# Work on the first and last item of a batched attention and graph-convolution kernel, moved between engines and queue positions

## The chip, the cores and the metric

The kernel runs on one core of a Trainium2 chip. A core has five engines, each with its own instruction queue, which it works through in order: TensorE (PE, matrix products, with PEld for its weight loads), VectorE (DVE), ScalarE (ACT), GpSimd (POOL) and SyncE (SP), which here only starts transfers. They meet through semaphores. The metric is the device time of one execution in microseconds (us); lower is better.

## The reference

There are 32 items of 512 rows and 512 columns, one adjacency matrix of 512 x 512 shared by all, three projections, a weight and biases. Each item goes through masked attention with 8 heads of 64 columns, a residual addition and a layer norm without gain, then through a graph convolution, another residual addition and another layer norm:

```python
q = (x @ Wq + bq).reshape(b, n, H, HD)          # the same for k and v
scores = jnp.einsum('bihd,bjhd->bhij', q, k) / jnp.sqrt(HD)
scores = scores + jnp.where(adj == 0, -1e9, 0.0)
out = jnp.einsum('bhij,bjhd->bihd', softmax(scores), v)
x = layernorm(x + out)
norm_adj = adj * deg_inv_sqrt[:, None] * deg_inv_sqrt[None, :]
x = layernorm(x + einsum('nm,bmo->bno', norm_adj, x @ W1) + b1)
```

## The kernel before

Everything is in the function `unshifted`; the function `general` behind it runs only if a flag, counted at the end, says that the softmax without a running maximum lost accuracy. All engines are wrapped so that their instructions stay in the order in which the program issues them. The profile gives the wrapper's line, L40, for all of these, so the operations are told apart by the names of their tiles.

*Products.* Each of the three projections is done as seven block products instead of eight (`seven`): the weight and the transposed item are kept as four 256-row or 256-column parts and three further sums and differences. `weigh` makes those of a weight (four operations on 128x512 elements), `turns` transposes an item in two halves on VectorE (`turn`, tile xT from x) and then makes the item's combinations (`combine`, four operations; on VectorE for the first item, on GpSimd for all later ones). The products go in the order (0,0), (1,1), (5,5), (6,6), (4,4), (3,2), (2,3), part of the weight first, part of the item second. So the first two need no combination, and the third needs the second result of `weigh` and of `combine`. Each piece is eight TensorE instructions of 256 columns into one of three PSUM buffers (mm), which VectorE or ScalarE must empty. `values_of(b)` gives the values of an item, `keys_and_queries(b, r)` for r = 0, 1 its keys and queries, in which each piece holds four instructions for wk and four for wq.

*Attention.* An item has eight steps: four pairs of heads, two halves of keys. A step k issues `scores` of step k (eight TensorE instructions into two PSUM buffers sc, then on VectorE a minimum and the mask, on ScalarE the exponent, on GpSimd the sum over keys in acc) and `values` of step k-1 (eight instructions into av; VectorE transposes every second one into yb, and small transfers bring it into yT). The exponents lie in four buffers named e. One holds until its value product and its GpSimd sum are done. `sums` turns acc into column sums (sT) with small matmuls after half of the heads and after all of them.

*After the attention.* `finish(b)` is a list of 19 pieces: the reciprocals of the sums, four scalings of yT on VectorE with residual additions on GpSimd (yT from xr), four statistics, the root on GpSimd, and then for each of four row blocks the norm, a high part hi on ScalarE, a low part lo on VectorE and the addition of the bias on GpSimd. `convolve(b)` is a list whose first four pieces (the first factor, 8 instructions each, with hi and lo against adjT) give zT, and whose other eight are the four second factors (8 instructions against w) with their norm and their stores.

*Order.* The main loop runs over all 256 steps and two more. From the third step of each item on, a list `side` of pieces is spread over eight steps: the projections of the next item, `finish` and `convolve` of the one before, and the transposes of the one after next. A piece carries a cost, and `run(side, share)` issues pieces until their costs reach the share that is due. `weave(side, main)` spreads one list between the pieces of another. Pieces of `finish` have the cost 0, except the first with 0.6, so a list of nothing else is not spread: all but its first piece waits for the last step, where the share is 1. That is what happens in the last item:

```python
            else:
                side, late = finish(b - 1), convolve(b - 1)
...
    run(weave(finish(B - 1), late))
    run(convolve(B - 1))
```

So in the last item's attention TensorE has scores and values alone; then come the rest of item 30's `finish`, then item 31's `finish` woven into item 30's `convolve`, and last item 31's `convolve`. The flag is counted behind all that.

At the start the program issues, in this order: the transposes and combinations of item 0; the additional parts of Wv on VectorE; the value and key biases; the parts of Wk on GpSimd; item 0's values; the scale of 1/8 on Wq and its parts on VectorE; item 0's keys and queries; the transposes of item 1; then `adjacency`, which in four rounds transposes the adjacency matrix on TensorE and makes from it on VectorE the mask (maskT), a rounded copy (adjT), and a check (off, lost), and last the degrees (deg, root, dis). Then the steps begin. A buffer holds one half of an item before its transposition (x), so the load of the second half of item 1 can begin only when the first is transposed. The adjacency matrix lies in one of two yT buffers until the degrees are read from it.

Of the kernel before, what the change touches and what calls it, by code (L numbers as in the profile page):

```python
# [9 lines left out]
F32 = mybir.dt.float32  # L10
# [3 lines left out]
AF = mybir.ActivationFunctionType  # L14
ALU = mybir.AluOpType
AX = mybir.AxisListType

P = 128
# [3 lines left out]
MASKED = -1e9  # L22
# [23 lines left out]
def unshifted(  # L46
# [25 lines left out]
    nc = tc.nc  # L72
    B, N, D = x.shape
    NT = N // P
    DT = D // P
    G = H // 2
    SCALE = 1.0 / HD**0.5
    tensor, vector, scalar, gpsimd = (InOrder(tc, e) for e in (nc.tensor, nc.vector, nc.scalar, nc.gpsimd))
# [53 lines left out]
    def load_parts(w, name, engine):  # L132
        t = consts.tile([P, 7, 2, HALF], F32, name=name)
        for i in range(2):
            for q in range(4):
                engine.dma_start(
                    t[32 * q : 32 * (q + 1), 2 * i : 2 * i + 2].rearrange("r j u o -> r (j u) o"),
                    w[ts(q, P), ts(i, HALF)].rearrange("(t r) o -> r t o", r=32),
                )
        return t  # L140

    def weigh(t, engine):
        engine.tensor_tensor(t[:, 4], t[:, 2], t[:, 3], ALU.add)
        engine.tensor_tensor(t[:, 5], t[:, 4], t[:, 0], ALU.subtract)
        engine.tensor_tensor(t[:, 6], t[:, 0], t[:, 2], ALU.subtract)
        engine.tensor_tensor(t[:, 2], t[:, 1], t[:, 5], ALU.subtract)
# [3 lines left out]
        nc.sync.dma_start(t, w.rearrange("(t p) o -> p t o", p=P))  # L150
        return t

    def load_row(v, name):
        t = consts.tile([P, v.shape[0]], F32, name=name)
        nc.sync.dma_start(t, bass.AP(tensor=v.tensor, offset=v.offset, ap=[[0, P], [1, v.shape[0]]]))
        return t

    def load_column(v, name):
        t = consts.tile([P, DT], F32, name=name)
        nc.sync.dma_start(t, v.rearrange("(t p) -> p t", p=P))  # L160
        return t

    load_x(0, 0)
    load_x(0, 1)
    wv = load_parts(Wv, "wv", nc.scalar)
    bk_c = load_column(bk, "bk_c")
    bq_c = load_column(bq, "bq_c")
    wk = load_parts(Wk, "wk", nc.sync)
    wq = load_parts(Wq, "wq", nc.sync)
    bv_r = load_row(bv, "bv_r")  # L170
    adj_sb = acts.tile([P, NT, N], F32, name="yT")
    nc.sync.dma_start(adj_sb, adj.rearrange("(t p) o -> p t o", p=P))
    w1 = load_weight(W1, "w1")
    b1_r = load_row(b1, "b1_r")

    ident = consts.tile([P, P], F32, name="ident")
    make_identity(nc, ident)
# [9 lines left out]
    dis = consts.tile([P, NT], F32, name="dis")  # L187
    lost = consts.tile([P, NT], F32, name="lost")

    def adjacency():  # L190

        for m in range(NT):
            p = ps_mm.tile([P, N], F32, name="mm")
            for n in range(NT):
                tensor.transpose(p[:, ts(n, P)], adj_sb[:, n, ts(m, P)], ident)
            vector.tensor_scalar(maskT[:, m, :], p, 0.0, MASKED, op0=ALU.is_equal, op1=ALU.mult)
            vector.tensor_copy(adjT[:, m, :], p)
            off = work.tile([P, N], F32, name="off", tag="e", bufs=4)  # L200
            vector.tensor_tensor(off, p, adjT[:, m, :], ALU.not_equal)
            vector.tensor_reduce(lost[:, m : m + 1], off, AX.X, ALU.add)
        deg = consts.tile([P, NT], F32, name="deg")
        vector.tensor_reduce(deg, adj_sb, AX.X, ALU.add)
        pos = consts.tile([P, NT], F32, name="pos")
        vector.tensor_scalar(pos, deg, 0.0, None, op0=ALU.is_gt)
        safe = consts.tile([P, NT], F32, name="safe")
        vector.tensor_scalar(safe, deg, TINY, None, op0=ALU.max)
        root = consts.tile([P, NT], F32, name="root")
        gpsimd.tensor_tensor(root, safe, minus_half, ALU.pow)  # L210
        vector.tensor_mul(dis, root, pos)
# [44 lines left out]
    def values_of(b):  # L256


        def multiply(p, i, j):
            for r in range(2):  # L260
                for u in range(2):
                    tensor.matmul(
                        p[:, r, :], XT[b][:, j, u, ts(r, P)], wv[:, i, u, :],
                        start=u == 0, stop=u == 1,
                    )

        def first(e1, p):
            V[b] = acts.tile([P, NT, D], F32, name="v")
            vector.tensor_add(e1, p, bv_r[:, None, :HALF].to_broadcast([P, 2, HALF]))

        def middle(u2, u1, p):
            vector.tensor_add(u2, u1, p)
            vector.tensor_add(u2, u2, bv_r[:, None, HALF:].to_broadcast([P, 2, HALF]))

        def out(i, j):
            return V[b][:, 2 * j : 2 * j + 2, ts(i, HALF)]

        return seven(multiply, first, middle, out)

    def keys_and_queries(b, r):  # L280


        def multiply(p, i, j):
            for c, w in enumerate((wk, wq)):
                for u in range(2):
                    tensor.matmul(
                        p[:, c, :], w[:, i, u, ts(r, P)], XT[b][:, j, u, :],
                        start=u == 0, stop=u == 1,
                    )

        def first(e1, p):
            for g in (r, r + 2):
                KQ[b, g] = acts.tile([P, 2, N], F32, name="kq", bufs=5)
            for c in range(2):
                scalar.activation(e1[:, c], p[:, c], AF.Identity, bias=bias[:, c, r : r + 1], scale=1.0)

        def middle(u2, u1, p):
            for c in range(2):
                vector.scalar_tensor_tensor(
                    u2[:, c], u1[:, c], step[:, c, r : r + 1], p[:, c], op0=ALU.add, op1=ALU.add  # L300
                )

        def out(i, j):
            return KQ[b, r + 2 * i][:, :, ts(j, HALF)]

        return seven(multiply, first, middle, out)

    def turns(b):

        return [(0, turn, (b, 0))], [(0, turn, (b, 1))] + [(0, combine, (b, k)) for k in range(4)]  # L310
# [145 lines left out]
    def weave(side, main):  # L456

        out, done = [], 0
        for k, piece in enumerate(main):
            due = len(side) * (k + 1) // len(main)  # L460
            out += side[done:due] + [piece]
            done = due
        return out + side[done:]
# [39 lines left out]
    def run(pieces, share=1.0):  # L503

        due = share * sum(c for c, _, _ in pieces)
        done = 0
        while pieces and (done < due or share == 1.0):
            c, f, args = pieces.pop(0)
            f(*args)
            done += c  # L510
# [2 lines left out]
    steps = [(b, g, jj) for b in range(B) for g in ORDER for jj in range(2)]  # L513
    S = len(steps)
    PER = 2 * G
    for piece in sum(turns(0), []):
        piece[1](*piece[2])
    weigh(wv, vector)
    value_biases()
    biases()  # L520
    if B > 1:
        load_x(1, 0)
    weigh(wk, gpsimd)
    run(values_of(0))
    vector.tensor_scalar(wq[:, :4], wq[:, :4], SCALE, None, op0=ALU.mult)
    weigh(wq, vector)
    run(keys_and_queries(0, 0))
    run(keys_and_queries(0, 1))
    run(sum(turns(1), []) if B > 1 else [])
    adjacency()  # L530
    side, late = [], []
    for k in range(S + 2):
        b, at = divmod(k, PER)
        if at == 2:
            run(side)
            if b:
                for i in range(NT):
                    load_residual(b - 1, i)
            if b + 2 < B:
                load_x(b + 2, 0)  # L540
            side = []
            if b + 1 < B:
                side = values_of(b + 1) + keys_and_queries(b + 1, 0) + keys_and_queries(b + 1, 1)
            if b == 0:
                side = side + (sum(turns(2), []) if B > 2 else [])
            elif b < B - 1:
                chain = finish(b - 1)
                side = chain[:1] + side[:1] + weave(chain[1:], side[1:])
                one, two = turns(b + 2) if b + 2 < B else ([], [])
                conv = convolve(b - 1)  # L550
                side = side + one + conv[:4] + weave(two, conv[4:])
            else:
                side, late = finish(b - 1), convolve(b - 1)
        if k >= 2:
            pb, pg, pj = steps[k - 2]
            if pj == 1 and pg in ORDER[1::2]:
                sums(pb, ORDER.index(pg) // 2)
        if k < S:
            scores(steps[k])
        if 1 <= k <= S:  # L560
            values(steps[k - 1])
        run(side, 1.0 / (PER - (at - 2) % PER))
# [1 line left out]
    for i in range(NT):  # L564
        load_residual(B - 1, i)
    run(weave(finish(B - 1), late))
    run(convolve(B - 1))

# [8 lines left out]
    tensor.matmul(p, count, ones, start=True, stop=True)  # L579
    bad = small.tile([1, 1], I32, name="bad")  # L580
    vector.tensor_scalar(bad, p, -1.0, float(P * B * NT * H), op0=ALU.mult, op1=ALU.add)
    return nc.values_load(bad, min_val=0, max_val=P * B * NT * H + N * N)


# [280 lines left out]
```

## Time and profile before

| quantity | value |
|---|---|
| median of three runs | 3025.76 us (3025.0 to 3026.0) |
| span of the profiled execution | 3025.3 us |
| TensorE busy | 2957.3 us, 98% |
| VectorE busy | 2188.4 us, 72% |
| GpSimd busy | 1557.6 us, 51% |
| ScalarE busy | 775.9 us, 26% |
| mean granted TensorE clock | 0.988 |
| mean HBM traffic | 35 GB/s |

Busy time is the time in which an engine has an instruction in work. A share of the span is a mean over stages of different kinds, and the first and the last item differ from the 30 between. The page also gives the span in 40 equal slices of 75.6 us, with one digit for each (tenths, 9 for 90% or more), and the clock that TensorE was granted. Timeline rows give the start, the duration (for merged rows that from the first to the last instruction), the engine, the operation, its tiles, the count, and in brackets the idle time ahead with what ended it.

### The profile page before, as it was taken

The page shows a single profiled execution, that of the slowest core. Times are in us where ns is not written, and L with a number is a line of the kernel's source. Part 1 is how long each engine was busy: PE and PEld are TensorE (multiplying, and loading weights), DVE is VectorE, ACT ScalarE, POOL GpSimd, SP SyncE. Part 2 cuts the span into 40 slices and gives each one's busy share as a digit, 9 for nine tenths or more (in the row PEclk, how much of TensorE's full clock was granted, in tenths as well). Part 3 has the DMA queues.
Part 4 walks back from the last instruction along what each step waited for, and adds up shares of the span by engine and source line. Part 5 has one row for each costly group of instructions (what it writes and reads, how often), then busy time and mean ns, then how long its engine had stood idle before and what let it go on. Part 6 is the DMA issues. An engine that isn't in the chain of part 4 may idle for free.

```text
span 3025.3 us, 33347 instructions
## 1 busy us (share of the span) xinstructions
PE 2957.3 (98%) x12178; PEld 1721.9 (57%) x12178; DVE 2188.4 (72%) x3146; ACT 775.9 (26%) x929; POOL 1557.6 (51%) x939
## 2 busy tenths in 40 slices
PE   6899999999999999999999999999999999999996
PEld 5465555655555655556655556555556555556533
DVE  5577767777767777767877767877677777677756
ACT  0222222222222222222222222222222222222231
POOL 1355554555544555554555455555545555445553
PEclk8999999999999999999999999999999999999997
DMA  5012221122221112211222211122211222211121
GB/s 125 11 29 53 53 56 28 42 49 53 53 53 28 46 46 56 53 42 32 50 48 56 53 32 41 46 53 53 56 28 42 49 53 53 54 28 46 40 51 40
DMA packets 382861, 142.28 MB, mean 47 GB/s; under 512 B 280032, under 2 KB 348640, under 8 KB 382688
## 3 DMA queue, kind: packets, MB, share of 16 engines
q1 hardware_dynamic: 381536, 139.01, 19.8%
q8 instruction: 98, 1.61, 0.2%
q10 hardware_dynamic: 1152, 1.05, 0.2%
q14 instruction: 75, 0.61, 0.1%
HBM read 72.88 MB, written 33.55 MB: 35 GB/s over the span
## 4 chain that ended last, share of the span: by engine, by line
PE 96%; DVE 2%; DMA 1%; POOL 1%; issue 0%; SPq 0%; ACT 0%; DVEq 0%; POOLq 0%; ACTq 0%
PE mm L40 64%; PE sc L40 16%; PE av L40 15%; DMA x<-in_x_dram 1%; POOL acc L40 0%; DVE yT L40 0%; DVE st L40 0%; DVE e L40 0%; DVE ob L40 0%; DVE lo L40 0%; DMA bv_r<-in_L_gnn_bv_dram 0%; POOL rstd L40 0%; DMA wq<-in_L_gnn_Wq_dram 0%; SPq L105 0%; DVE xT L40 0%
## 5 line engine op out<-in xcount | busy, mean ns | idle before, releaser
L40 ACT ACTIVATE e<-e 128x1024 f32<-128x1024 f32 x512 | 541.2, 1057 | 1375.8 <-DVE e L40 1357.1
L40 POOL TENSOR_TENSOR acc<-acc,e 128x1024 f32<-128x1024 f32 x256 | 635.1, 2481 | 465.6 <-ACT e L40 455.4
L40 DVE SCALAR_TENSOR_TENSOR e<-sc,maskT 128x1024 f32<-128x1024 f32 x512 | 601.6, 1216 | 291.4 <-PE sc L40 290.2
L40 POOL TENSOR_TENSOR acc<-e 128x1024 f32<-128x1024 f32 x128 | 311.3, 2432 | 580.7 <-ACT e L40 529.9
L40 PE MATMUL sc<-kq 64*128 64x512 f32 x2048 | 512.6, 619 | 8.8 <-DVE e L40 8.8
L40 PE MATMUL av<-e,v 128*64 128x512 f32 x2048 | 496.6, 606 | 0.0
L40 PE MATMUL mm<-xT,wk 128*128 128x256 f32 x1792 | 469.8, 385 | 0.0
L40 PE MATMUL mm<-xT,wq 128*128 128x256 f32 x1792 | 460.0, 379 | 1.1 <-DVE wq L40 1.1
L40 PE MATMUL mm<-w,zT 128*128 128x512 f32 x1024 | 455.8, 598 | 0.0
L40 PE MATMUL mm<-wv,xT 128*128 128x256 f32 x1792 | 410.8, 387 | 19.2 <-DVE xT L40 9.5
L40 PEld LDWEIGHTS mm<-xT,wk 128*128 128x128 f32 x1792 | 332.6, 190 | 118.5 <-DVE e L40 26.8
L40 PEld LDWEIGHTS mm<-wv,xT 128*128 128x128 f32 x1792 | 338.8, 193 | 95.4 <-DVE u L40 23.5
L40 PEld LDWEIGHTS mm<-xT,wq 128*128 128x128 f32 x1792 | 340.4, 190 | 47.7 <-DVE wq L40 1.5
L40 PEld LDWEIGHTS mm<-w,zT 128*128 128x128 f32 x1024 | 189.6, 190 | 264.1 <-issue 237.5
L40 PEld LDWEIGHTS sc<-kq 64*128 64x128 f32 x2048 | 177.1, 187 | 264.3 <-issue 204.8
L40 PEld LDWEIGHTS av<-e,v 128*64 128x64 f32 x2048 | 124.2, 136 | 341.9 <-issue 315.4
L40 DVE SCALAR_TENSOR_TENSOR ob<-mm,dis,yT 128x512 f32<-128x512 f32 x128 | 96.1, 751 | 223.4 <-PE mm L40 223.3
L40 POOL TENSOR_TENSOR rstd<-ve,minus_half 128x1 f32<-128x1 f32 (+1 forms) x160 | 116.8, 730 | 217.7 <-DVE ve L40 214.3
L40 PE MATMUL mm<-adjT,hi 128*128 128x512 f32 x512 | 207.6, 406 | 10.3 <-ACT hi L40 10.3
L40 PE MATMUL mm<-adjT,lo 128*128 128x512 f32 x512 | 204.8, 400 | 7.4 <-DVE lo L40 7.4
L40 POOL TENSOR_TENSOR yT<-yT,b_r 128x512 f32<-128x512 f32 x128 | 170.5, 1332 | 78.3 <-DVE lo L40 78.3
L40 POOL TENSOR_TENSOR xT<-xT 128x512 f32<-128x512 f32 x124 | 158.7, 1280 | 53.5 <-DVE xT L40 51.0
(71 smaller groups left out, 2329.6 us busy)
## 6 DMA issues: line engine op xcount, KB each, us to landing
x<-in_x_dram SPq DMA_DIRECT2D x256, 128.0 KB, 2.9
xr<-in_x_dram SPq DMA_DIRECT2D x128, 256.0 KB, 2.7
yT<-yb SPq DMA_DIRECT2D x512, 64.0 KB, 2.4
out_dram<-ob SPq DMA_DIRECT2D x128, 256.0 KB, 2.0
wv<-in_L_gnn_Wv_dram ACTq DMA_DIRECT2D x8, 128.0 KB, 4.8
wk<-in_L_gnn_Wk_dram SPq DMA_DIRECT2D x8, 128.0 KB, 4.1
wq<-in_L_gnn_Wq_dram SPq DMA_DIRECT2D x8, 128.0 KB, 4.4
yT<-in_adj_dram SPq DMA_DIRECT2D x1, 1024.0 KB, 7.4
```

The lines of the kernel that those rows point to most:

```text
L40: return self.tc.keep_in_program_order(op(*args, **kwargs))
```

## The change

At the start, the additional parts of Wv are made on GpSimd, ahead of those of Wk; the scaling of Wq is done on ScalarE; the value bias is loaded through ScalarE's queue behind Wv, instead of SyncE's queue behind Wq, and its difference and the other biases are made after the first two value pieces; the parts of Wq are made behind the first key piece. The four rounds of `adjacency` are woven between the pieces of the second half of keys and queries, and the degrees become a piece of their own in the first item's side list. The second half of item 1's transposes and its combinations are issued behind the first scores.

At the end, the pieces of item 30's `finish` get a cost of 0.5 each, so that they spread over the attention of item 31, followed by the four first-factor pieces of its `convolve`. The second-factor pieces are held back until after the attention, with item 31's `finish` woven between them. The flag's count is placed ahead of item 31's `convolve`. The aim is to give TensorE work where it waits.

```diff
     load_x(0, 1)
     wv = load_parts(Wv, "wv", nc.scalar)
+    bv_r = load_row(bv, "bv_r", nc.scalar)
...
-    bv_r = load_row(bv, "bv_r")
...
-    def adjacency():
-        for m in range(NT):
-            p = ps_mm.tile([P, N], F32, name="mm")
...
+    def adjacency(m):
+        p = ps_mm.tile([P, N], F32, name="mm")
...
+    def degrees():
         deg = consts.tile([P, NT], F32, name="deg")
...
-    for piece in sum(turns(0), []):
-        piece[1](*piece[2])
-    weigh(wv, vector)
+    weigh(wv, gpsimd)
+    run(sum(turns(0), []))
+    weigh(wk, gpsimd)
+    scalar.activation(wq[:, :4], wq[:, :4], AF.Copy, scale=SCALE)
+    first = values_of(0)
+    run(first[:2])
     value_biases()
     biases()
     if B > 1:
         load_x(1, 0)
-    weigh(wk, gpsimd)
-    run(values_of(0))
-    vector.tensor_scalar(wq[:, :4], wq[:, :4], SCALE, None, op0=ALU.mult)
+    run(first[2:])
+    masks = [(0, adjacency, (m,)) for m in range(NT)]
+    first = keys_and_queries(0, 0)
+    run(first[:1])
     weigh(wq, vector)
-    run(keys_and_queries(0, 0))
-    run(keys_and_queries(0, 1))
-    run(sum(turns(1), []) if B > 1 else [])
-    adjacency()
+    run(first[1:])
+    run(weave(masks, keys_and_queries(0, 1)))
+    one, two = turns(1) if B > 1 else ([], [])
+    run(one)
...
             if b == 0:
-                side = side + (sum(turns(2), []) if B > 2 else [])
+                side = side[:7] + [(0, degrees, ())] + side[7:] + (sum(turns(2), []) if B > 2 else [])
...
             else:
-                side, late = finish(b - 1), convolve(b - 1)
+                conv = convolve(b - 1)
+                side = [(0.5, *piece[1:]) for piece in finish(b - 1)] + conv[:4]
+                late = conv[4:]
...
             scores(steps[k])
+        if k == 0:
+            run(two)
...
     run(weave(finish(B - 1), late))
-    run(convolve(B - 1))
...
     vector.tensor_scalar(bad, p, -1.0, float(P * B * NT * H), op0=ALU.mult, op1=ALU.add)
+    run(convolve(B - 1))
     return nc.values_load(bad, min_val=0, max_val=P * B * NT * H + N * N)
```

More of the change, by code (lines that the diff above doesn't have):

```diff
@@ L151, in load_weight, with load_row @@
         return t
-    def load_row(v, name):
+    def load_row(v, name, engine):
         t = consts.tile([P, v.shape[0]], F32, name=name)
-        nc.sync.dma_start(t, bass.AP(tensor=v.tensor, offset=v.offset, ap=[[0, P], [1, v.shape[0]]]))
+        engine.dma_start(t, bass.AP(tensor=v.tensor, offset=v.offset, ap=[[0, P], [1, v.shape[0]]]))
         return t
@@ L173, in unshifted @@
     w1 = load_weight(W1, "w1")
-    b1_r = load_row(b1, "b1_r")
+    b1_r = load_row(b1, "b1_r", nc.sync)
     ident = consts.tile([P, P], F32, name="ident")
@@ L188, in unshifted @@
     lost = consts.tile([P, NT], F32, name="lost")
-    def adjacency():
-        for m in range(NT):
-            p = ps_mm.tile([P, N], F32, name="mm")
[L196 to L202, printed above, removed]
+    def adjacency(m):
+        p = ps_mm.tile([P, N], F32, name="mm")
+        for n in range(NT):
+            tensor.transpose(p[:, ts(n, P)], adj_sb[:, n, ts(m, P)], ident)
+        vector.tensor_scalar(maskT[:, m, :], p, 0.0, MASKED, op0=ALU.is_equal, op1=ALU.mult)
+        vector.tensor_copy(adjT[:, m, :], p)
+        off = work.tile([P, N], F32, name="off", tag="e", bufs=4)
+        vector.tensor_tensor(off, p, adjT[:, m, :], ALU.not_equal)
+        vector.tensor_reduce(lost[:, m : m + 1], off, AX.X, ALU.add)
+    def degrees():
         deg = consts.tile([P, NT], F32, name="deg")
```

## The prediction

> **What bounds the kernel now.** I read the page's busy times first, then the slices, then the busy times of stretches that I cut at the places where the slices fall, and last the timeline of those stretches. The page:
>
> ```profile
> PE 2957.3 (98%) x12178; PEld 1721.9 (57%) x12178; DVE 2188.4 (72%) x3146; ACT 775.9 (26%) x929; POOL 1557.6 (51%) x939
> ...
> PE   6899999999999999999999999999999999999996
> ...
> PEclk8999999999999999999999999999999999999997
> ```
>
> TensorE is busy for 98% of the span and sits idle for 3025.3 - 2957.3 = 68 us in all. From the third slice to the last but one it never drops below 9. So whatever is changed in the 30 middle items is worth nothing unless it slows TensorE; the change can only earn in the first 95 us and the last 110 us. The stretches (columns: stretch, its length, busy us of PE, PEld, DVE, ACT, POOL with the number of instructions, granted clock, DMA share, GB/s):
>
> ```profile
> 0.00:9.00 9.00, 0.00 (x0) 0.00 (x0) 0.85 (x1) 0.00 (x0) 0.97 (x10) 1.00 0.89 168
> 9.00:38.30 29.30, 21.18 (x60) 16.21 (x60) 17.90 (x25) 1.10 (x1) 6.49 (x4) 0.77 0.99 235
> 38.30:61.70 23.40, 23.39 (x108) 20.58 (x109) 11.80 (x19) 1.86 (x5) 0.00 (x0) 1.00 0.00 1
> 61.70:95.00 33.30, 16.49 (x57) 6.10 (x55) 23.03 (x29) 5.38 (x6) 13.12 (x8) 0.69 0.13 32
> 2915.60:2943.50 27.90, 25.33 (x108) 7.05 (x104) 17.03 (x19) 13.27 (x13) 21.20 (x9) 1.00 0.34 69
> 2943.50:2962.00 18.50, 5.49 (x14) 2.36 (x15) 16.09 (x29) 2.78 (x4) 10.77 (x8) 0.60 0.24 68
> 2962.00:2992.30 30.30, 24.71 (x65) 13.62 (x63) 25.17 (x49) 5.24 (x8) 15.91 (x13) 0.84 0.05 18
> 2992.30:3015.40 23.10, 22.99 (x59) 13.07 (x59) 8.35 (x17) 2.35 (x4) 5.12 (x5) 0.87 0.10 39
> ```
>
> At the head TensorE loses 9 us to the first loads, 8 us in the value products (9 to 38), and 17 us between 61.7 and 95, where VectorE makes the masks. The clock column says that the work beside those gaps also runs slowly. At the tail 13 us are lost where the norm of item 30 runs alone (2943.5 to 2962), 6 us beside the norm of item 31, and 10 us behind the last product. The timeline shows what each head gap waits for:
>
> ```profile
> 26.36 10.03 PE L40 MATMUL mm<-wv,xT 128*128 128x256 f32 x32 [3.16 <-DVE e L40]
> ...
> 68.18 1.25 DVE L40 STREAM_TRANSPOSE xT<-x 128x1024 f32<-128x1024 f32 x1 [4.42 <-DMA x<-in_x_dram]
> 69.35 0.65 DVE L40 TENSOR_SCALAR maskT<-mm 128x512 bf16<-128x512 f32 x1
> ...
> 71.47 1.09 PE L40 MATMUL mm<-ident,yT 128*128 128x128 f32 x4 [8.15 <-DVE off L40]
> ...
> 72.49 3.79 PE L40 MATMUL sc<-kq 64*128 64x512 f32 x8
> ...
> 83.66 2.35 DVE L40 SCALAR_TENSOR_TENSOR e<-sc,maskT 128x1024 f32<-128x1024 f32 x2
> ...
> 84.93 3.79 PE L40 MATMUL sc<-kq 64*128 64x512 f32 x8 [8.66 <-DVE e L40]
> ...
> 91.27 1.99 PE L40 MATMUL sc<-kq 64*128 64x512 f32 x8
> ```
>
> The reader is to see VectorE as one queue in which everything stands in line: the second turn of item 1 waits 4.42 us for its load, the four masks behind it wait too, and the first softmax step (83.66) behind those. The eight score matmuls take 3.79 us after each gap and 1.99 us later.
>
> **What the Trainium skill says.** "TensorE: Matmul & The Clock Gate", Part 1: about 3.4 us without work drop the array's clock to half, and about as much work restores it. The trace agrees: 3.79 against 1.99 us for one and the same group after gaps of 8.15 and 8.66 us. "SBUF — State Buffer", Who interferes with whom: a VectorE operation with two SBUF inputs and a GpSimd operation that reads SBUF exclude each other. The trace agrees in part: the four differences of Wv on VectorE took 0.69 to 1.76 us while GpSimd worked on Wk, the same operation on Wq with GpSimd idle 0.69 us. "TensorE: Matmul & The Clock Gate", Part 1, also has VectorE and ScalarE as strict first-in-first-out; the chain above behaves so.
>
> **The head, part by part.** (1) Wv to GpSimd, bv on the other DMA queue. VectorE loses 4.76 us of Wv work. The last Wv load is issued at 7.8 us and lands within 3.2 to 5.6 us, so GpSimd starts near 13; at the 1.65 us of the Wk rows it is done near 19.6, and its second result, which the third value piece needs, near 16.3. VectorE's four x combinations (2.75 us alone, from 15.3) now run beside that; with exclusion they end at 19 to 21 instead of 18.0. The third piece starts near 17.5 (was 19.4); bv no longer arrives at 23.8, so the first eviction comes at about 20 to 21 (was 25.6) and the fourth piece at about 21 (was 26.4). The rest took 9.7 us, from 26.36 to 36.0, partly at half clock; with a shorter gap ahead I take 8.5 us: the keys start at 29.5 instead of 36.0.
> (2) Scaling Wq on ScalarE. The row for 128x2048 is 1.22 us on VectorE; for ScalarE no row exists: 1.06 us for 1024 columns and 0.42 for 256 give about 2 us. ScalarE is idle to 37 us, so this costs nothing, and the stall of 1.05 us before the queries goes. The Wq differences (2.75 us) follow the first key product, hidden by two pieces of 1.72 us. Wk on GpSimd ends near 26.5, before its first use near 33.
> (3) First half of keys and queries: 7 pieces of 1.72 us, 29.5 to 41.5.
> (4) Second half with the masks between. TensorE has 12.0 us plus 16 transposes, about 2 us. VectorE has four masks of 2.75 us (11.0) and seven evictions of about 0.7 (5.0): 16.0 us from about 43.9, so VectorE sets the end, at 59.9. The second half took 11.6 us before, so weaving costs 4 to 5 us here, and removes 21 us later.
> (5) First turn of item 1 (1.25): softmax from 61.2, against 83.66. The second turn now stands behind the first scores. Its load begins only after the first turn and needs 4.4 us and an issue, so VectorE waits until about 65.8, then turns, and the second scores are masked from 67.1 (was 87.06). GpSimd's four combinations (5.2 us) stand behind the first sum; they are wanted near 75 and done near 72. The exponents of the second step end at 70.6 and its value products at 72.5, which ended at 95.05: 22.5 us earlier. TensorE idles some 3 to 4 us at 58 to 62 and may cool: I take off 1 us. Head: 21.5 us.
> (6) Degrees, 2.3 us and five small operations, go into item 0's steady part, where VectorE has a quarter of its time free and their result is first used an item later: nothing.
>
> **The tail.** (7) The norm of item 30 (19 pieces) now runs beside the attention of item 31, and its four first factors follow in the last four steps. GpSimd decides this: from 2919.1 to 2943.5 it does nine sums of 2.36 us, 21.2 us with only 3.2 us of gaps. Four residual additions of 1.30, one root of 1.02 and four bias additions of 1.33 add 11.5 us. Queued behind them are the sums of exponents, and behind those the four score buffers (VectorE) and the column sums (TensorE). So the last column sums go from 2943.5 to at least 2955.0; I take 2956.5. Then 1.05 + 1.8 (the last first factor, 8 x 0.228) + 0.66 + 0.34 us bring the reciprocals of item 31 to 2960.4, where they were at 2961.98. All the 18.5 us of lonely norm are thus mostly repaid in a longer attention: 1.6 us earned.
> (8) The norm of item 31 beside the second factors. VectorE: four scalings of 1.40, four statistics of 1.01, four evictions with statistics of 1.77, three stores of 0.54, 0.56 of judging, four norms of 0.54 to 1.15, four splits of 0.74 to 0.90: 24 to 27 us, plus about 1.6 us for the first second factor and 1 us for the root. I take 28, where it took 30.3: 2.3 us earned.
> (9) The flag's count goes ahead of the last convolution. Its matmul waits for VectorE (a store and three small operations, 1.2 us) and all 32 matmuls of the first factors stand behind it; before, 7 of them had run by the last split. 1.2 + 7 x 0.228 = 2.8 us lost. Behind the last store the 0.6 us from count to flag are saved. Tail: 1.6 + 2.3 - 2.8 + 0.6 = 1.7 us.
>
> **Sum:** 3025.8 - 21.5 - 1.7 = 3002.6, say 3002.5.
>
> **Rivals.** A, the above. B: the tail pays as it was meant to. If GpSimd's additions fall into its gaps and behind waits, and the last norm needs VectorE's 24 us alone, the tail earns 10 to 12 us: about 2992. For it: TensorE idles 13 us there; against: 21.2 of 24.4 us of GpSimd are taken. C: the tail costs. Two-input scalings on VectorE shut out the sums (means of 1.40 instead of 0.69 show it), the attention of item 31 ends at 2960 or later and TensorE goes cold before the last convolution: 5 to 7 us lost, about 3010. D: the head is bound by its loads. The DMA share is 0.99 to 38 us; if Wv or bv lands as late as before and the masks wait for the adjacency, only the 8 to 10 us at 62 to 84 remain: 3015 to 3020, no change to speak of. E, slower: the head earns nothing, because the second turn's wait moves onto the first softmax steps and all their products run at half clock, and the tail loses the 11.5 us in full: about 3035. Against it: the masks' 11 us are then still done beside products.
>
> **How the numbers follow.** A 0.60, B 0.20, C 0.13, D 0.04, E 0.03. The range takes A with its unknowns (keys start 28 to 31, attention end 2955 to 2959) and reaches to B and C: 2991 to 3012. Faster by more than 0.2% means under 3019.7: A, B, C and part of D, 0.95; within 0.02; slower 0.03.
>
> **What would show it.** Head right: keys start near 29.5 us, VectorE without gaps from 44 to 60, the first softmax step near 61, the second turn waiting some 4 us for its load, and value products of the second step ending near 72.5. Tail right: GpSimd busy without gaps in the last attention, the last column sums some 13 us later in that stage, and the norm of item 31 beginning about 1.6 us earlier relative to the stage's start. A long TensorE gap before the last convolution shows step 9. If TensorE in the middle items shows gaps that are not there now, all of this is wrong.

## The result and the profile after

| kernel | median | runs | ratio to before, 95% interval |
|---|---|---|---|
| before | 3025.92 us | 6 (3025.0 to 3027.36) | |
| changed | 3005.45 us | 6 (3002.76 to 3006.53) | 0.9931 (0.9918 to 0.9944) |

The change saves about 20.5 us, 0.7%. The profiled executions differ by 21.3 us (spans of 3025.3 and 3004.0). The page after, busy times and slices:

```profile
PE 2949.8 (98%) x12178; PEld 1720.2 (57%) x12178; DVE 2190.6 (73%) x3141; ACT 777.2 (26%) x930; POOL 1561.5 (52%) x943
...
PE   7999999999999999999999999999999999999986
...
PEclk9999999999999999999999999999999999999998
```

The first slice went from 6 to 7 and the second from 8 to 9, and the first one's clock from 8 to 9; at the end the last slice but one fell from 9 to 8, while the last one's clock rose from 7 to 8. TensorE now idles 3004.0 - 2949.8 = 54.2 us instead of 68. The saving is larger than that difference of 14 us, since the work beside the closed gaps also runs faster (TensorE is busy 7.5 us less with the same 12178 instructions). The busy times of stretches of the changed kernel, cut at its own stages (columns as in the prediction):

```profile
9.00:29.90 20.90, 17.10 (x57) 13.60 (x58) 16.91 (x18) 3.20 (x2) 11.60 (x8) 0.92 1.12 259
29.90:43.70 13.80, 13.80 (x65) 12.13 (x64) 8.19 (x13) 0.84 (x2) 0.00 (x0) 1.00 0.44 109
43.70:57.30 13.60, 12.62 (x67) 10.64 (x65) 12.52 (x21) 0.84 (x2) 0.00 (x0) 1.00 0.00 1
57.30:72.00 14.70, 11.63 (x42) 3.23 (x41) 11.65 (x12) 5.72 (x6) 7.28 (x5) 0.88 0.29 72
2893.70:2938.60 44.90, 34.43 (x128) 11.85 (x124) 39.17 (x46) 17.11 (x19) 35.59 (x18) 0.89 0.29 65
2938.60:2942.20 3.60, 3.60 (x22) 2.35 (x22) 0.69 (x2) 1.02 (x2) 0.00 (x0) 1.00 0.53 73
2942.20:2971.70 29.50, 13.70 (x32) 5.71 (x30) 23.64 (x53) 2.92 (x5) 14.92 (x13) 0.82 0.08 32
```

**Head.** From 29.9 to 57.3 us TensorE works almost without a gap, from 44 us on beside VectorE making the masks; the value products of item 0's second step end, and item 1's products begin, at 71.99 instead of 95.06: 23.1 us earlier. The timeline of the changed kernel at that place:

```profile
21.20 8.86 PE L40 MATMUL mm<-wv,xT 128*128 128x256 f32 x32 [1.99 <-DVE e L40]
...
59.70 1.24 DVE L40 STREAM_TRANSPOSE xT<-x 128x1024 f32<-128x1024 f32 x1
60.86 2.31 DVE L40 SCALAR_TENSOR_TENSOR e<-sc,maskT 128x1024 f32<-128x1024 f32 x2
...
62.10 3.21 PE L40 MATMUL sc<-kq 64*128 64x512 f32 x8 [2.84 <-DVE e L40]
...
65.52 1.25 DVE L40 STREAM_TRANSPOSE xT<-x 128x1024 f32<-128x1024 f32 x1 [2.35 <-DMA x<-in_x_dram]
66.69 2.32 DVE L40 SCALAR_TENSOR_TENSOR e<-sc,maskT 128x1024 f32<-128x1024 f32 x2
```

The reader is to see the two waits that stood here, 8.15 us for the check of the adjacency and 8.66 us for the softmax, gone or cut to 2.84 us, and the wait of the second turn (2.35 us) now behind the first softmax step.

**Middle.** The lead of 23.1 us has become 21.8 by 200 us and is 21.9 at the last item. Both kernels have one wait of TensorE there, about 3 us, before a group of 16 products; the group took 5.26 us before and 6.59 after, so 1.3 us were lost. The experiments show below that this length varies with no change in the code.

**Tail.** The softmax of the last item's third step begins 21.9 us earlier (2915.62 and 2893.71), and the end comes 21.3 us earlier. So the tail costs 0.6 us. Cut at the starts of the named operations, for the last split at its end:

| from, to | before | changed | earned |
|---|---|---|---|
| third step's softmax, reciprocals of item 31 | 46.4 us | 48.5 | -2.1 |
| reciprocals, last split of item 31 | 30.9 | 27.9 | 3.1 |
| last split, last eviction | 22.4 | 26.0 | -3.5 |
| last eviction, end | 10.0 | 8.0 | 2.0 |

The waits of TensorE in the changed kernel, by what ended them (us in total, times, longest), and three rows of the tail's timeline:

```profile
PE mm L40 <- DVE ones L40: 15.8, 1, 15.8
PE sc L40 <- DVE e L40: 12.6, 6, 5.8
PE mm L40 <- DVE xT L40: 10.8, 2, 9.6
PE mm L40 <- DVE inv L40: 3.0, 1, 3.0
```

```profile
2896.98 6.79 DVE L40 TENSOR_TENSOR yT<-yT,inv 128x512 f32<-128x512 f32 x4
...
2904.95 3.78 PE L40 MATMUL sc<-kq 64*128 64x512 f32 x8 [5.84 <-DVE e L40]
...
2971.72 0.19 PE L40 MATMUL mm<-ones,count 128*1 128x1 f32 x2 [15.82 <-DVE ones L40]
```

Before, the longest wait of the tail was 10.3 us for the high parts; it is 15.8 us for the flag's count now. And the waits for softmax (e), 8.8 us before and nearly all of it in the head, are 12.6 us, of which 5.84 and 2.86 are new, in the last item's attention. The eight scores behind these two waits took 3.78 and 3.21 us instead of 1.99.

### The profile page after: what moved, and what is told of

Read it like the earlier page. It is cut to its first block, busy times and chain, and to the rows that moved or that the text cites. A ratio compares the mean times of both kernels' runs of the same rounds, so it can differ in the third digit from the quotient of the medians.

```text
span 3004.0 us, 33348 instructions
## 1 busy us (share of the span) xinstructions
PE 2949.8 (98%) x12178; PEld 1720.2 (57%) x12178; DVE 2190.6 (73%) x3141; ACT 777.2 (26%) x930; POOL 1561.5 (52%) x943
## 4 chain that ended last, share of the span: by engine, by line
PE 96%; DVE 2%; DMA 1%; issue 0%; POOL 0%; SPq 0%; ACT 0%; DVEq 0%; POOLq 0%; ACTq 0%
PE mm L40 65%; PE sc L40 16%; PE av L40 16%; DMA x<-in_x_dram 1%; DVE yT L40 1%; DVE e L40 0%; DVE xT L40 0%; DVE lo L40 0%; DVE ob L40 0%; DVE st L40 0%; POOL rstd L40 0%; SPq L105 0%; DVE kq L40 0%; DVE off L40 0%; DVE mv L40 0%
## 5 line engine op out<-in xcount | busy, mean ns | idle before, releaser
L40 PE MATMUL sc<-kq 64*128 64x512 f32 x2048 | 513.9, 620 | 12.6 <-DVE e L40 12.6
L40 PE MATMUL mm<-wv,xT 128*128 128x256 f32 x1792 | 409.1, 387 | 15.8 <-DVE xT L40 10.8
L40 POOL TENSOR_TENSOR yT<-yT,xr 128x512 f32<-128x512 f32 x128 | 163.3, 1287 | 41.5 <-DVE yT L40 25.8
```

The costliest lines, as they stand in the source:

```text
L40: return self.tc.keep_in_program_order(op(*args, **kwargs))
```

## The experiments

Every kernel but the one with the tail alone is the changed one with the edit shown; ratios are to the kernel before, timed on the same chip, where its median lies between 3026.09 and 3026.46 us for all rows.

| run | median (runs from, to) | ratio, 95% interval |
|---|---|---|
| start alone | 3003.12 us (3001.76 to 3003.65) | 0.9923 (0.9909 to 0.9937) |
| tail alone | 3027.57 (3025.72 to 3029.95) | 1.0004 (0.9996 to 1.0013) |
| flag in the middle | 3002.15 (3001.31 to 3003.07) | 0.9921 (0.9908 to 0.9935) |
| last sums on TensorE | 3007.39 (3005.64 to 3009.42) | 0.9935 (0.9922 to 0.9949) |
| masks in a lump | 3010.26 (3008.84 to 3011.61) | 0.9945 (0.9931 to 0.9959) |
| Wv on VectorE | 3003.28 (3001.12 to 3004.9) | 0.9924 (0.9911 to 0.9938) |
| two factors held back longer | 3003.47 (3001.55 to 3004.28) | 0.9923 (0.9909 to 0.9936) |
| scalings spread | 3008.49 (3007.65 to 3010.71) | 0.9943 (0.9929 to 0.9956) |
| changed kernel again | 3004.54 (3004.38 to 3005.42) | 0.9929 (0.9916 to 0.9943) |
| early load | 3002.41 (3002.3 to 3004.82) | 0.9925 (0.9911 to 0.9938) |
| four edits together | 2995.66 (2992.52 to 2997.7) | 0.9902 (0.9887 to 0.9917) |
| the same, item 2's turn earlier | 2995.97 (2995.65 to 2996.89) | 0.9901 (0.9886 to 0.9916) |

The changed kernel's two medians lie 0.9 us apart, so a difference of 1 us between two rows is not told from chance; 2 us and more are taken as real where the runs do not overlap.

**Start alone: the end of the kernel before.**

```diff
-                conv = convolve(b - 1)
-                side = [(0.5, *piece[1:]) for piece in finish(b - 1)] + conv[:4]
-                late = conv[4:]
+                side, late = finish(b - 1), convolve(b - 1)
...
+    run(convolve(B - 1))
...
-    run(convolve(B - 1))
```

> The changed start with the tail of before. Theory (the start earned all of it, the tail's parts cancel): as fast as the changed kernel within 2 us, 3004 to 3007 us, and the first softmax step at 60.9 us as there. Rival (the tail earned a part, and the middle lost some of the start's 23 us): 3010 us or more.

3003.12 us, 1.4 to 2.3 us faster than the whole change.

**Tail alone: the start of the kernel before**, with `adjacency` whole, all turns of item 1 ahead of the steps, Wv on VectorE and the old order of loads:

> The start of before with the changed tail, the early flag included. Theory: within 2.5 us of the kernel before, 3023 to 3027 us; in the trace the attention of the last item some 17 us longer, the norm of item 31 some 3 us shorter, some 2 us saved behind the last store. Rival (the tail earned 5 us or more, hidden in the changed kernel by losses in the middle): 3021 us or less.

3027.57 us, no different from before. So the start earns everything, and the tail nothing or a little less. The trace of the start alone has the reciprocals of item 31 at 46.4 us after the third step's softmax, as before; the tail alone has them at 48.5 us, as the changed kernel's first profile. The changed kernel run again has them at 49.9 us; why is shown under the last sums.

**Flag in the middle.** The count is issued behind the first factors of item 31 instead of ahead of them.

```diff
+    conv = convolve(B - 1)
+    run(conv[:4])
...
-    run(convolve(B - 1))
+    run(conv[4:])
```

> The changed kernel with the flag's count between the first and the second factors of the last convolution instead of ahead of it. Theory of the prediction's step 9 (the flag's matmul holds up TensorE by 1.2 us and by seven products that could have run before): 2 to 3 us faster than the changed kernel. Rival (the product that waits for the last split sets the start, and a TensorE that has idled runs at half clock in either order): under 1 us faster.

2.4 to 3.3 us faster than the changed kernel. From the last split to the last eviction it took 22.7 us, against 24.6 to 26.0 us in the eight profiles that have the flag ahead and all second factors woven in (changed, again, tail alone, last sums, lump, Wv on VectorE, early load, scalings spread). With the flag behind everything it was 22.4 us before and 21.8 with the start alone. Its timeline shows products beside the splits, where the changed kernel's TensorE stood:

```profile
2960.73 0.79 PE L40 MATMUL mm<-adjT,hi 128*128 128x512 f32 x1 [6.12 <-ACT hi L40]
...
2964.43 0.80 PE L40 MATMUL mm<-adjT,lo 128*128 128x512 f32 x1 [1.69 <-DVE lo L40]
...
2977.35 0.19 PE L40 MATMUL mm<-ones,count 128*1 128x1 f32 x2
```

The last row has no bracket: the count no longer waits, and no product stands idle behind it.

**Last sums on TensorE.** To test whether GpSimd ends the last attention, its two sums of exponents of the last step are left to TensorE, which adds them in the column sums.

```diff
+        elif s == steps[-1]:
+            REST[b, g] = E[s]
...
+            parts = [ACC[b, g]] + REST.get((b, g), [])
+            for n, part in enumerate(parts):
```

> The changed kernel, with the last two sums of exponents (4.8 us of GpSimd) done by TensorE inside the column sums: eight small products more. Theory of the prediction's step 7 (GpSimd's last sum sets the end of the last attention): the column sums come some 4 us earlier, 3 us faster than the changed kernel after about 1 us for the products. Rival (by then TensorE itself sets it: in the changed kernel the column sums begin at 2938.62 us without any wait, behind the third first-factor piece): no gain, or 1 us slower.

It got no faster: 3007.39 us, 1.9 to 2.9 us slower. GpSimd's last sum ended 4.9 us earlier in the stage than in the changed kernel, but the column sums began 46.6 us after the third step's softmax, where the changed kernel has 44.9 and, run again, 46.3. Then they took longer. In the changed kernel itself the column sums start with no wait, right behind the third first factor, 0.4 us after GpSimd's last sum:

```profile
2933.35 4.84 POOL L40 TENSOR_TENSOR acc<-acc,e 128x1024 f32<-128x1024 f32 x2
...
2938.29 0.40 PE L40 MATMUL mm<-adjT,lo 128*128 128x512 f32 x1
2938.62 1.07 PE L40 MATMUL mm<-acc,sel 128*32 128x512 f32 x8
```

So GpSimd's last sum is near the limit, but taking it away moves nothing. What stands ahead is VectorE. The last scores of the item wait for it, in the changed kernel and in its repeat:

```profile
2928.59 2.26 PE L40 MATMUL sc<-kq 64*128 64x512 f32 x8 [0.63 <-DVE e L40]
```

```profile
2928.06 3.58 PE L40 MATMUL sc<-kq 64*128 64x512 f32 x8 [0.63 <-DVE e L40]
```

The three groups of scores that wait for VectorE start 11.2, 25.0 and 34.9 us after the third step's softmax, within 0.05 us, in the eleven profiles that have the changed tail and the scalings not spread. The same eight products take from 2.26 to 3.79 us there, and the starts do not move. So up to 34.9 us VectorE's queue sets the pace. From the last scores to the column sums TensorE is then busy all the time, and its clock makes the difference: 10.03 us at a granted clock of 1.00 in the changed kernel, 11.39 us at 0.85 in the repeat. The reciprocals come at 48.5 us where the last scores took 2.26 us (changed, tail alone, Wv on VectorE) and at 49.9 or 50.0 where they took 3.21 to 3.66 (seven others).

The twelve scalings, norms and splits of item 30 (groups of VectorE in the changed kernel, 2893.7 to 2938.6; busy us and mean ns behind the bar):

```profile
L40 DVE TENSOR_TENSOR yT<-yT,inv 128x512 f32<-128x512 f32 x4 | 6.8, 1756 | 0.0
L40 DVE TENSOR_SCALAR yT<-yT,mv,rstd 128x512 f32<-128x512 f32 x4 | 6.1, 1556 | 0.0
L40 DVE SCALAR_TENSOR_TENSOR lo<-yT,dis,hi 128x512 fp32r<-128x512 f32 x4 | 6.0, 1519 | 0.0
```

They took 18.9 us. Before, from the same point to the reciprocals of item 31, they took 4.6 + 2.1 + 4.9 = 11.6 us. The 7.3 us more stand beside GpSimd's sums and additions, and the softmax steps queue behind them (5.84 and 2.86 us of new TensorE waits).

**Scalings spread.** The four scalings get twice the share each, so that softmax steps come between them.

```diff
-                side = [(0.5, *piece[1:]) for piece in finish(b - 1)] + conv[:4]
+                side = [(1.1 if 1 <= n <= 4 else 0.5, *piece[1:]) for n, piece in enumerate(finish(b - 1))] + conv[:4]
```

> The changed kernel with the four scalings of item 30 spread over two steps (cost 1.1 instead of 0.5). Theory (in the changed kernel the four scalings, shut out by GpSimd, hold up the softmax behind them for 6.8 us, and TensorE, waiting 5.84 us, goes to half clock): [...]the eight score products after it at 1.99 us instead of 3.78, last column sums 2 to 5 us earlier, whole as much faster. Rival (the same work has to be done before the column sums, wherever it stands): under 1 us.

3 to 4 us slower. TensorE's waits in this run:

```profile
PE mm L40 <- DVE lo L40: 7.5, 4, 2.8
PE sc L40 <- DVE e L40: 7.1, 4, 2.8
```

The wait for softmax shrinks from 12.6 to 7.1 us, its longest from 5.8 to 2.8, and a wait of 7.5 us for the splits, 0.9 in the changed kernel, takes its place: TensorE stands in the first factors until VectorE has made their low parts. The column sums came 49.1 us after the third step's softmax. Spreading the scalings also puts the later pieces of the norm further back, and they must be done before the first factors.

**Two factors held back longer.** Item 30's last second factor pieces stay behind item 31's norm.

```diff
-    run(weave(finish(B - 1), late))
+    run(weave(finish(B - 1), late[:3]))
+    run(late[3:])
```

> The changed kernel with only the first two second-factor pieces woven into the norm of item 31 and the other two issued behind it. Theory (in this stage VectorE's queue is the path, and each second factor puts 1.8 us of eviction and statistics and a store of 0.54 in front of the norm): the last split comes 4 us earlier, whole 3 to 4 us faster than the changed kernel. Rival (GpSimd's additions and roots or the buffers set it): under 1 us.

From the reciprocals to the last split 20.4 us instead of 27.9: two of the four evictions, with their statistics and stores, no longer stand between the steps of the norm on VectorE. But the kernel gains only 1 to 2 us, no more than chance can give; the flag's count now stands behind those evictions:

```profile
2960.38 2.42 DVE L40 SCALAR_TENSOR_TENSOR lo<-yT,dis,hi 128x512 fp32r<-128x512 f32 x2
...
2970.10 0.19 PE L40 MATMUL mm<-ones,count 128*1 128x1 f32 x2 [13.99 <-DVE ones L40]
```

The last split is done at 2962.80, and the first factors start only behind the count, at 2970.22.

**Masks in a lump** (`run(keys_and_queries(0, 1) + masks)` in place of the weave):

> The changed kernel with the four mask rounds in one block behind the second half of keys and queries, all else as changed. Theory (VectorE's queue sets the first softmax step, so what counts is how much of the masks' 11 us stands beside products): products of that half end near 55.5 us, the masks after them near 67, first softmax step near 67 instead of 60.9, value products of the second step 4 to 7 us later than 72.0, with TensorE at half clock; whole 3009 to 3013 us. Rival (the gain came from the earlier values and from the second turn's place, not from the weave): within 2 us of the changed kernel.

5 to 6 us slower; the first softmax step came at 66.45 instead of 60.86 us, with a wait of TensorE of 8.27 us ahead of the next scores. The weave is worth that much. Even so, this first softmax step comes 17.2 us earlier than before (83.66): most of what the head gained there does not depend on the weave.

**Wv on VectorE again**, behind the combinations, the rest of the new start kept (`run(sum(turns(0), []))`, then `weigh(wv, vector)`):

> The changed kernel with the sums and differences of Wv back on VectorE, behind the combinations, bv still early. Theory of the prediction's step 1 (part of the 6 us won in the values comes from GpSimd taking Wv, part from the early bv): the keys start at 31 to 34 us instead of 29.9, and all later stages as much later; 2 to 4 us slower than the changed kernel. Rival (combinations and Wv exclude each other on the two engines anyhow, so the place doesn't matter): keys at 30 us, within 1 us.

No loss: 3003.28 us, keys from 29.32 us instead of 29.89. Two rows of VectorE in this run, then two of the changed kernel:

```profile
14.46 2.75 DVE L40 TENSOR_TENSOR xT<-xT 128x512 f32<-128x512 f32 x4
17.12 2.74 DVE L40 TENSOR_TENSOR wv<-wv 128x512 f32<-128x512 f32 x4
```

```profile
13.62 6.29 POOL L40 TENSOR_TENSOR wv<-wv 128x512 f32<-128x512 f32 x4 [11.99 <-DMA wv<-in_L_gnn_Wv_dram]
14.24 6.21 DVE L40 TENSOR_TENSOR xT<-xT 128x512 f32<-128x512 f32 x4
```

VectorE alone does both in 5.5 us. Side by side, each engine needs over 6.2 us for one of them. In this run TensorE then does the last five value pieces without a gap, from 18.59 us; before, it stood 3.16 us ahead of the last four, until VectorE had the bias (23.86 us) and could empty a buffer.

**Early load.** The second half of item 1 is loaded at once, into a buffer (zT) that is free until item 0's convolution.

```diff
+        elif b == 1 and j == 1:
+            X[b, j] = acts.tile([P, 2, 8, DT, 32], F32, name="zT", bufs=1)[:, 0]
...
-        if j == 0 and b:
+        if j == 0 and b > 1:
...
+        load_x(1, 1)
```

> The changed kernel with the second half of item 1 loaded into a buffer that is free until the first convolution, so that its load waits for nothing. Theory (VectorE stands 2.35 us before the second turn for this load, and the second softmax step behind it): no such wait, second softmax step at 64.3 us instead of 66.7, 1.5 to 3 us faster than the changed kernel. Rival (the value products of item 1 wait for GpSimd's combinations, or for the exponents, just as long): under 1 us.

The wait of 2.35 us went and the second softmax step came 2.84 us earlier, at 63.85, but item 1's products began only 1.06 us earlier: TensorE, at half clock (3.65 us for the eight scores), was then the slower one. The whole took 3002.41 us, 2.1 to 3.0 us faster with overlapping runs; no more than the 1.06 us is shown for this edit, as its profile also has the shortest time of the group shown next (3.69 us).

**The changed kernel again:**

> The changed kernel unaltered, on the chip of the next three, as their measure: 3003 to 3007 us.

3004.54 us. It also bears on the middle. The group of 16 products behind the 3 us wait, in the changed kernel, in its repeat and with the flag in the middle:

```profile
149.23 6.59 PE L40 MATMUL mm<-wv,xT 128*128 128x256 f32 x16 [3.02 <-DVE inv L40]
```

```profile
149.82 5.38 PE L40 MATMUL mm<-wv,xT 128*128 128x256 f32 x16 [3.02 <-DVE inv L40]
```

```profile
149.22 3.69 PE L40 MATMUL mm<-wv,xT 128*128 128x256 f32 x16 [2.99 <-DVE inv L40]
```

The same code up to that point, the same wait within 0.03 us, and 3.69 to 6.59 us. So the 1.3 us lost in the middle need no cause in the change, and up to 3 us of any single profile here are this draw.

**Four edits together:** Wv on VectorE, the early load, the held-back pieces and the flag in the middle.

> Four edits at once on the changed kernel: Wv back on VectorE, the early load of item 1's second half, two second factors held behind the norm of item 31, the flag's count between the last first and second factors. Theory (with two second factors held back the last split already came 7 us earlier, 2962.8 instead of 2970.1, but the flag's matmul waited behind their evictions; with the flag out of the way those 7 us come through): 7 to 9 us at the tail and 2 to 4 at the start, 2993 to 2997 us. Rival (the gains only add as measured singly, 2 + 3 + 2 + 2 us, or less): 2997 to 3001 us.

2995.66 us, 9 us faster than the changed kernel and 30 faster than before. The profiled execution is the fastest of its four (span 2990.7); there the last split ends at 2959.43, 20.4 us after the reciprocals, and the first factors have begun at 2952.44. The count waits for nothing:

```profile
2957.01 2.42 DVE L40 SCALAR_TENSOR_TENSOR lo<-yT,dis,hi 128x512 fp32r<-128x512 f32 x2
...
2968.60 0.19 PE L40 MATMUL mm<-ones,count 128*1 128x1 f32 x2
```

From the reciprocals to the end it takes 51.7 us, against 61.8 and 60.6 in the two profiles of the changed kernel, 59.5 with the pieces held back alone and 58.6 with the flag moved alone. So the two tail edits, 1 to 3 us each alone in these profiles, bring 9 to 10 together there: the early end of the norm is of use only when the flag does not stand ahead of the first factors. Counted from the third step's softmax the tail is 8.8 and 8.9 us shorter than in those two profiles, as much as the medians gain in all, so the two edits at the start are not shown to add anything.

**Item 2's turn earlier.** On top of these, item 2's second turn and its combinations, with the next load behind them, are moved ahead into item 1's side list, to remove the wait at 149 us.

> The one before with the second half of item 2's turn and its combinations issued behind the second value piece of item 2 instead of at the end of item 0's list. Theory (in both kernels TensorE waits 3.0 us near 149 or 172 us while VectorE stands before this load, and then works 1 to 3 us at half clock): the wait falls below 3 us or goes, 2 to 4 us faster than the one before. Rival (the third value piece then waits for GpSimd's combinations just as long): within 1 us.

The same time. The wait has only changed its name:

```profile
148.72 5.41 PE L40 MATMUL mm<-wv,xT 128*128 128x256 f32 x16 [4.68 <-POOL xT L40]
```

TensorE now waits for GpSimd's combinations, and longer (4.68 us).

## Why the prediction was right, and where it was not

The predicted 3002.5 us lies 2.9 us under the measured 3005.45, inside the range, and case A is what the total shows. But the head gave more than A said and the tail less: in the profiles 23.1 - 1.2 (middle) - 0.6 = 21.3 us, where A had 21.5 + 1.7 = 23.2. That the total came so near is in part luck: errors of +1.6 us at the head, -1.2 in the middle and -2.3 at the tail partly cancel.

- *Steps 1 to 6, the head:* 21.5 us predicted, 23.1 measured at item 1's products (22.5 in the repeat). Event by event: fourth value piece 21 against 21.20, keys 29.5 against 29.89, first turn 59.9 against 59.70, first softmax 61.2 against 60.86, second scores masked 67.1 against 66.69, value products done at 72.5 against 71.99. The 1 us taken off for cooling was not needed: TensorE stood 2.84 us and did cool (eight scores took 3.21 us instead of 1.99; in the repeat, behind the same wait, 2.26), but beside the second turn's wait. The scaling on ScalarE took 1.92 us against the 2 that were estimated, and was hidden. The degrees cost nothing that the trace shows.
- *Step 1's reason was wrong although its times were right.* It credited VectorE with 4.76 us of Wv work given away. The run with Wv back on VectorE starts the keys no later. The 4.76 us were themselves stretched by GpSimd's Wk work; alone they are 2.74 us, and what the move saves is paid back by the combinations (6.21 us instead of 2.75; their end, put at 19 to 21, came at 20.45). The earlier keys come from the rest of the new start; the traces point to the early bias, but no run changes it alone.
- *Step 4's weave* was to cost 4 to 5 us in the second half of keys and queries and to remove 21 us later. It cost 3.2 us there (15.3 us from 41.98 to 57.27, and 12.1 before, from 49.63 to 61.72, which the prediction took as 11.6). But the lump shows the weave to be worth 5 to 6 us in all. The rest of the 22.8 us by which the first softmax step comes earlier is mostly in the earlier keys (6.3), the second turn behind the first scores (its 4.42 us of wait and 1.25 of work) and the degrees taken out of the way (3.8).
- *Step 7 is the one that failed.* It said "GpSimd decides this" and earned 1.6 us; measured are 2.1 us lost (48.5 us in the place of 46.4), an error of 3.7 us, and 3.5 us lost in the repeat. The column sums came 44.9 and 46.3 us after the third step's softmax, 17.0 and 18.4 later in the stage than before, where 13 were predicted (2956.5 - 2915.6 = 40.9). The owner was wrong: the run with GpSimd's last sums removed gained nothing; VectorE's queue, whose norm operations stretched from 11.6 to 18.9 us, delays the softmax steps, up to the same 34.9 us in all eleven profiles of that tail, and TensorE then works the rest off without a gap. GpSimd has its part through VectorE, whose operations it slows. No run takes the norm off VectorE with the rest of the tail kept. The prediction had priced the scalings at 1.40 us only in step 8 and had left VectorE's queue out of step 7. Rival C came nearest: an attention that ends "at 2960 or later" is what came (2915.6 + 44.9 = 2960.5). But it let GpSimd's sums wait for the scalings, and it is the softmax steps that did; and its 5 to 7 us are too many.
- *Step 8* was right in time: 27.9 us where 28 were given; 3.1 us earned instead of 2.3, as the stretch before was 30.9 and not 30.3.
- *Step 9* was right in mechanism and near in size: 2.8 us predicted, 3.5 between the two profiles, 2.1 to 3.5 over the eight profiles with the flag ahead. The flag in the middle takes it back. Its second term was mis-sized: from the last eviction to the end 2.0 us were saved, not 0.6 (10.0 us in both profiles with the flag behind everything, 7.9 to 8.1 in all others). What the rest of these 2 us is was not tried.
- *The middle:* no new gap, as foretold; the 1.3 us lost there lie within the draw shown above.

Rival B, a tail that pays 10 to 12 us, is not this change. Two more edits come near it: in the profile of the four edits the tail takes 101.5 us from the third step's softmax to the end, against 109.7 before, 8.2 us less.

## What to carry to other kernels

Before work is moved into an engine's idle time, list whose queue each of its operations joins and who stands behind it there; of VectorE and GpSimd, the one that is fuller by its mean (GpSimd here, 21.2 of the 27.9 us of the last attention before) is not always the one that delays the next product. Moving Wv's sums from VectorE to GpSimd earned nothing, as VectorE worked on two SBUF inputs at the same time. A small product at the head of an in-order queue, such as this count, costs what everything behind it could have done meanwhile, and an edit that looks worthless (1 to 2 us) can be worth much more once such a block is gone, so it is worth trying the promising ones together too.

## What the runs showed of the hardware

- **VectorE and GpSimd side by side do little more than one after the other.** Four two-input operations of 128x512 took 2.75 us on VectorE alone and 6.21 us beside four such on GpSimd (6.29 us). The eight together took 6.83 us (13.62 to 20.45); one after the other they would take 2.75 + 5.21 = 7.96 us, with the 5.21 us that GpSimd needs for four while VectorE works on operations with one SBUF input. The norm's tensor_scalar with one input is slowed too: a mean of 540 ns before, 1556 ns beside GpSimd's sums. The Trainium skill, "SBUF — State Buffer", Who interferes with whom, says that tensor_scalar can enter two-port modes and then contends; this trace agrees.
- **A gap of 3.0 us can lower the clock, for a varying length of time.** Behind waits of 2.82 to 3.16 us the 16 products took 5.10 to 6.73 us in eleven profiles and 3.69 us in two (waits of 2.99 and 3.03); the 16 products before them, without a wait, took 3.62 us. The Trainium skill, "TensorE: Matmul & The Clock Gate", Part 1, puts the idle time that lowers the clock at about 3.4 us and calls the window free-running. The variation agrees with a free-running window; the gap that suffices was shorter here, though the profile models where a product ends, and the measurement decides.
